# Self-attention's softmax halves exchanged by ScalarE copies instead of transfers

## The chip, the core and the metric

The kernel runs on one NeuronCore of a Trainium2 chip. The metric is the time of one execution on the device in microseconds. The engines are TensorE (matmuls; PE in the profile, PEld its weight loads), VectorE (DVE), ScalarE (ACT), GpSimd (POOL) and SyncE (SP), which here only issues DMA transfers. Each engine works through its own instructions in the order in which they were written; semaphores hold an instruction until what it needs is there.

## What is computed

One transformer block in float32 on x of 2 x 1024 x 256, with a context of 2 x 154 x 192: layer norm and self-attention with 16 heads of 64, layer norm and cross-attention to the context, layer norm and a gated feed-forward, each added to its input. Cut to what matters here:

```python
def _attention(xq, xkv, wq, wk, wv, wo, bo):
    q = (xq @ wq).reshape(B, S, N_HEADS, D_HEAD)
    k = (xkv @ wk).reshape(B, T, N_HEADS, D_HEAD)
    v = (xkv @ wv).reshape(B, T, N_HEADS, D_HEAD)
    attn = jnp.einsum('bihd,bjhd->bhij', q, k) * D_HEAD ** (-0.5)
    attn = jax.nn.softmax(attn, axis=-1)
    out = jnp.einsum('bhij,bjhd->bihd', attn, v).reshape(B, S, D_ATTN)
    return out @ wo + bo

h = _layernorm(x, ln1_g, ln1_b)
x = _attention(h, h, sa_wq, sa_wk, sa_wv, sa_wo, sa_bo) + x
h = _layernorm(x, ln2_g, ln2_b)
x = _attention(h, cond_emb, ca_wq, ca_wk, ca_wv, ca_wo, ca_bo) + x
h = _layernorm(x, ln3_g, ln3_b)
p = h @ ff_w1 + ff_b1
a, gate = p[..., :D_FF], p[..., D_FF:]
out = a * jax.nn.gelu(gate) @ ff_w2 + ff_b2 + x
```

## The kernel before

The order of the instructions on each engine is written out by hand: the program runs under a manual schedule, and each engine gets its instructions in the order in which the Python code emits them.

**Steps and units.** Self-attention runs in 16 units, one for each pair of heads (8) of each batch element (2). A unit has 8 steps; the loop over `p` counts all 128 of them. A step treats 128 queries of the pair, as two tiles of 64 queries. The 1024 keys are split into two halves, and the halves are laid on the partitions: in a tile of scores, 128 partitions by 2 heads by 512 keys, the partitions are four quarters of 32. Quarters 0 and 1 hold the same 32 queries with the first and the second half of the keys, quarters 2 and 3 the next 32 queries in the same manner (`scores`, line 476). So a softmax row lies in two neighbouring quarters, and its maximum and its sum have to be joined over both.

**The tile `st`.** For each step, `st` holds 128 partitions x [side, kind, tile, head], 2 x 2 x 2 x 2 numbers. Side 0 is what the partition's own half gave: kind 0 the negated maxima, kind 1 the sums of the exponents. Side 1 is to hold the same eight numbers of the neighbouring quarter (quarter a4 takes those of quarter a4 ^ 1). `st` has four buffers, so a step overwrites what the fourth step before it used.

**A step on the engines.** In the order of the program:

- TensorE computes the two score tiles (`s`, line 483) into two PSUM buffers, each of which can be overwritten as soon as the exponents have read it.
- VectorE takes the negated maxima of each tile (line 645, two instructions of 128 x 1024) into side 0.
- ScalarE computes the exponents (line 494, four instructions of 128 x 512, each with a read-out of the accumulated sum, which goes into side 0 as well).
- `scale_groups` of the step **before** starts with `join` (line 508). GpSimd forms the differences of the two sides' maxima (`dd`, lines 512 to 514), ScalarE their exponents (`ee`, line 516), GpSimd the joined sums (`zz`, line 518, and `den`, line 520).
- `exchange` (line 500) brings this step's side 0 to the neighbouring quarters' side 1. Its result is used by `join` one step later.
- VectorE transposes the weights of the step two before (line 609, two instructions of 128 x 1024), adds finished outputs to x in some steps (line 464), and then takes the reciprocal `rd` of the joined sums of the step before (line 591). GpSimd then scales that step's exponents by `rd` and `ee` (line 595, four instructions of 128 x 512).

The maxima of the next step are the next thing on VectorE, except that in some units the layer norm of a later stage puts statistics (lines 230 and 231) and an offset (line 246) between. On ScalarE, the instructions behind `ee` are evictions of projections or outputs from PSUM (lines 367, 375, 392, 630), and then the next step's exponents.

**TensorE's work of a step.** Behind its scores comes one of: the projection of the next unit's queries or keys (line 352) or values (line 383), a fourth of the weighted sum of the values of a finished unit half (line 530, 64 matmuls), or output projections (line 457) and small things.

**SyncE's queue.** It issues the weight loads (line 132), the regrouping of the values (lines 399 and 400), and the exchange's four transfers a step (line 504), 512 in all, each of 1 KB.

The closure in which the order of a step is written:

```python
def then():
    members = [exponents(f"{p}_{i}", sc[i], st, i) for i in range(2)]
    late = scale_groups(*joins.pop(0)) if joins else None
    exchange(st)
    joins.append((p, st, members))
    return late
```

Of the kernel before, what the change touches and what calls it, by code (L numbers as in the profile page):

```python
# [18 lines left out]
def tile_transformer_block(ctx: ExitStack, tc: tile.TileContext, a: dict, out: bass.AP):  # L19
    nc = tc.nc  # L20
# [19 lines left out]
    KB = 32  # L40
# [65 lines left out]
    for n in names[:2]:  # L106
        for r0 in range(0, P, HR):
            (nc.scalar if n == names[0] else nc.sync).dma_start(
                out=cols[r0:r0 + HR, row_of[n]:row_of[n] + NH],
                in_=w[n].rearrange("(r p) -> p r", p=HR),  # L110
# [365 lines left out]
    def scores(u, q, k, g):  # L476
        sc = ps_s.tile([P, 2, HB], F32, tag="s", name=f"s_{u}")
        for a4 in range(4):
            a2, h = divmod(a4, 2)
            for j in range(2):  # L480
                r = slice(j * DH, (j + 1) * DH)
                c = g * QG + a2 * KB
                nc.tensor.matmul(  # L483
                    sc[a4 * KB:(a4 + 1) * KB, j, :], lhsT=q[r, c:c + KB],
                    rhs=k[r, h * HB:(h + 1) * HB], start=True, stop=True,
                    tile_position=(j * DH, a4 * KB),
                )
        return sc

    def exponents(u, sc, st, i):  # L490

        pr = pp_.tile([P, 2, HB], F32, tag="P", name=f"p_{u}")
        for j in range(2):
            nc.scalar.activation(  # L494
                pr[:, j, :], sc[:, j, :], AF.Exp, bias=st[:, 0, 0, i, j:j + 1],
                accum_out=st[:, 0, 1, i, j:j + 1],
            )
        return pr

    def exchange(st):  # L500

        for a4 in range(4):
            o4 = a4 ^ 1
            nc.sync.dma_start(
                out=st[a4 * KB:(a4 + 1) * KB, 1], in_=st[o4 * KB:(o4 + 1) * KB, 0]
            )

    def join(u, st):

        dd = small.tile([P, 2, 4], F32, tag="dd", name=f"dd_{u}")  # L510
        neg = st[:, :, 0].rearrange("p s i j -> p s (i j)")
        nc.gpsimd.tensor_tensor(dd[:, 0, :], neg[:, 1, :], neg[:, 0, :], ALU.subtract)
        nc.gpsimd.tensor_tensor(dd[:, 1, :], neg[:, 0, :], neg[:, 1, :], ALU.subtract)
        nc.gpsimd.tensor_scalar(dd, dd, 0.0, 1.0, op0=ALU.min, op1=ALU.mult)
        ee = small.tile([P, 2, 4], F32, tag="ee", name=f"ee_{u}")
        nc.scalar.activation(ee, dd, AF.Exp)  # L516
        zz = small.tile([P, 2, 4], F32, tag="zz", name=f"zz_{u}")
        nc.gpsimd.tensor_tensor(zz, ee, st[:, :, 1].rearrange("p s i j -> p s (i j)"), ALU.mult)  # L518
        den = small.tile([P, 4], F32, tag="den", name=f"den_{u}")
        nc.gpsimd.tensor_tensor(den, zz[:, 0, :], zz[:, 1, :], ALU.add)  # L520
        return ee, den
# [63 lines left out]
    def scale_groups(u, st, members):  # L585

        ee, den = join(u, st)

        def reciprocals():
            rd = small.tile([P, 4], F32, tag="rd", name=f"rd_{u}")  # L590
            nc.vector.reciprocal(rd, den)  # L591
            for i, pr in enumerate(members):
                for j in range(2):
                    c = 2 * i + j
                    nc.gpsimd.tensor_scalar(  # L595
                        pr[:, j, :], pr[:, j, :], rd[:, c:c + 1], ee[:, 0, c:c + 1],
                        op0=ALU.mult, op1=ALU.mult,
                    )
                groups.append(pr)

        return reciprocals
# [35 lines left out]
    def self_first(p):  # L637

        b, pr = units[p // (2 * SH)]
        g = p % (2 * SH)  # L640
        q, k, _ = qk["sa", b, pr]
        st = small.tile([P, 2, 2, 2, 2], F32, tag="st8", name=f"st_{p}")
        sc = [scores(f"{p}_{i}", q, k, 2 * g + i) for i in range(2)]
        for i in range(2):
            nc.vector.tensor_reduce(st[:, 0, 0, i, :], sc[i], AX.X, ALU.max, negate=True)  # L645

        def then():
            members = [exponents(f"{p}_{i}", sc[i], st, i) for i in range(2)]
            late = scale_groups(*joins.pop(0)) if joins else None
            exchange(st)  # L650
            joins.append((p, st, members))
            return late

        return then
# [323 lines left out]
    with tc.manual_schedule():  # L978
# [93 lines left out]
        for c in range(CA):  # L1072
# [66 lines left out]
            elif n == 2:  # L1139
# [3 lines left out]
                elif ui == HP:  # L1143
                    wo["ca"] = const.tile([P, NPAIR, D], F32, tag="wo", name="ca_wo")
                    later[:0] = [lambda i=i: nc.sync.dma_start(
                        out=wo["ca"][:, i, :], in_=w["ca_wo"][i * P:(i + 1) * P, :])
# [65 lines left out]
```

## Time and profile before

| | us |
|---|---|
| median of 3 runs | 1120.16 (1119.69 to 1120.71) |
| the profiled execution | 1119.22 |
| its span, first to last instruction | 1117.4 |
| self-attention's steps, first maxima to last exponents | about 18.8 to 718.8 |

The stages follow one another: the first layer norm and projections up to about 18 us, the self-attention up to about 725 us (with the second layer norm beside it), then cross-attention, and the feed-forward to the end. The busy shares of the page's 40 slices (tenths; 9 is 90% or more; 28 us a slice):

```profile
PE   8999999999999999999999999999999999999998
DVE  4889999898998899999989989868777875412212
ACT  4666666766666666667666765665555553121111
POOL 2777777777777777777777777766656653220000
```

TensorE is busy throughout, VectorE nearly so in the first 26 slices, which are the self-attention; ScalarE and GpSimd are busy for about two thirds there. The costliest groups that have to do with the softmax, and the transfers of the exchange (after the count: busy time and mean duration in ns, then idle time of the engine ahead of them and what ended most of it; of a transfer: KB each, us to landing):

```profile
L494 ACT ACTIVATE p<-s,st 128x512 f32<-128x512 f32 x512 | 344.8, 686 | 199.0 <-DVE st L645 190.6
L595 POOL TENSOR_SCALAR p<-p,rd,ee 128x512 f32<-128x512 f32 x512 | 385.6, 768 | 47.6 <-DVE rd L591 46.3
L645 DVE TENSOR_REDUCE st<-s 128x2 f32<-128x1024 f32 x256 | 301.1, 1217 | 26.9 <-PE s L483 13.5
L609 DVE STREAM_TRANSPOSE pT<-p 128x1024 f32<-128x1024 f32 x256 | 302.2, 1218 | 0.3 <-POOL p L595 0.3
...
st<-st SPq DMA_DIRECT2D x512, 1.0 KB, 1.8
```

### The profile page before, as it was taken

The page shows a single profiled execution, that of the slowest core. Times are in us where ns is not written, and L with a number is a line of the kernel's source. Part 1 is how long each engine was busy: PE and PEld are TensorE (multiplying, and loading weights), DVE is VectorE, ACT ScalarE, POOL GpSimd, SP SyncE. Part 2 cuts the span into 40 slices and gives each one's busy share as a digit, 9 for nine tenths or more (in the row PEclk, how much of TensorE's full clock was granted, in tenths as well). Part 3 has the DMA queues.
Part 4 walks back from the last instruction along what each step waited for, and adds up shares of the span by engine and source line. Part 5 has one row for each costly group of instructions (what it writes and reads, how often), then busy time and mean ns, then how long its engine had stood idle before and what let it go on. Part 6 is the DMA issues. An engine that isn't in the chain of part 4 may idle for free.

```text
span 1117.4 us, 36668 instructions
## 1 busy us (share of the span) xinstructions
PE 1103.5 (99%) x14340; PEld 686.5 (61%) x14340; DVE 855.7 (77%) x1205; ACT 629.5 (56%) x2030; POOL 681.0 (61%) x1584
## 2 busy tenths in 40 slices
PE   8999999999999999999999999999999999999998
PEld 5445545545545455455455455476776777888887
DVE  4889999898998899999989989868777875412212
ACT  4666666766666666667666765665555553121111
POOL 2777777777777777777777777766656653220000
PEclk9999999999999999999999999999999999999999
DMA  3222212111111012011111111146665453000000
GB/s 85 70 57 50 55 27 51 48 34 41 32 31 42 22 41 46 13 42 39 24 41 32 31 32 26 25 95 158 160 157 125 114 115 79 10 11 10 20 10 19
DMA packets 102318, 59.14 MB, mean 53 GB/s; under 512 B 31994, under 2 KB 92930, under 8 KB 102146
## 3 DMA queue, kind: packets, MB, share of 16 engines
q1 hardware_dynamic: 100914, 56.15, 21.3%
q8 instruction: 113, 1.85, 0.7%
q10 hardware_dynamic: 1232, 0.66, 0.2%
q14 instruction: 59, 0.48, 0.1%
HBM read 27.12 MB, written 2.10 MB: 26 GB/s over the span
## 4 chain that ended last, share of the span: by engine, by line
PE 92%; ACT 2%; DVE 2%; DMA 1%; POOL 1%; SPq 1%; issue 1%; DVEq 0%; ACTq 0%; POOLq 0%
PE s L483 20%; PE po L530 20%; PE pa L933 10%; PE py_sa L457 5%; PE pv_sa L383 5%; PE py_ca L457 5%; PE pf L956 5%; PE pk_sa L352 4%; PE pq_sa L352 4%; PE pq_ca L352 4%; PE poc L851 4%; PE sc L772 3%; ACT p L494 2%; PE ph_ln L270 1%; PE pv_ca L733 1%; DVE st L645 1%
## 5 line engine op out<-in xcount | busy, mean ns | idle before, releaser
L494 ACT ACTIVATE p<-s,st 128x512 f32<-128x512 f32 x512 | 344.8, 686 | 199.0 <-DVE st L645 190.6
L595 POOL TENSOR_SCALAR p<-p,rd,ee 128x512 f32<-128x512 f32 x512 | 385.6, 768 | 47.6 <-DVE rd L591 46.3
L645 DVE TENSOR_REDUCE st<-s 128x2 f32<-128x1024 f32 x256 | 301.1, 1217 | 26.9 <-PE s L483 13.5
L609 DVE STREAM_TRANSPOSE pT<-p 128x1024 f32<-128x1024 f32 x256 | 302.2, 1218 | 0.3 <-POOL p L595 0.3
L483 PE MATMUL s<-k_sa,q_sa 64*32 64x512 f32 x4096 | 251.6, 594 | 5.0 <-ACT p L494 4.3
L530 PE MATMUL po<-pT,v_sa 64*64 64x256 f32 x4096 | 235.8, 380 | 0.9 <-DVE pT L609 0.9
L530 PEld LDWEIGHTS po<-pT,v_sa 64*64 64x64 f32 x4096 | 150.6, 133 | 109.3 <-issue 31.2
L483 PEld LDWEIGHTS s<-k_sa,q_sa 64*32 64x32 f32 x4096 | 66.8, 106 | 126.3 <-issue 68.2
L799 POOL TENSOR_SCALAR p<-p,rden 128x154 f32<-128x154 f32 x256 | 96.8, 399 | 76.0 <-DVE rden L796 75.6
L788 ACT ACTIVATE p<-sc,neg 128x154 f32<-128x154 f32 x256 | 96.1, 405 | 83.3 <-DVE rden L796 78.1
L942 DVE SCALAR_TENSOR_TENSOR u<-pa,cols,gate 128x256 f32<-128x256 f32 x64 | 31.0, 484 | 123.1 <-ACT gate L939 123.1
L933 PE MATMUL pa<-hT_ln,wf 128*128 128x256 f32 x512 | 121.1, 380 | 0.2 <-ACT p L788 0.2
L939 ACT ACTIVATE gate<-pa,cols 128x256 f32<-128x256 f32 x64 | 30.3, 474 | 147.8 <-PE pa L933 146.0
L933 PEld LDWEIGHTS pa<-hT_ln,wf 128*128 128x128 f32 x512 | 96.9, 190 | 13.9 <-issue 0.8
L494 ACT ACTIVATION_READ_ACCUMULATOR p<-s,st 128x1 f32 x512 | 103.8, 203 | 0.0
L383 PEld LDWEIGHTS pv_sa<-sa_wv,hT_ln 64*128 64x128 f32 x1024 | 58.8, 188 | 14.5 <-DMA st<-st 5.9
L518 POOL TENSOR_TENSOR zz<-ee,st 128x8 f32<-128x8 f32 x128 | 25.9, 202 | 65.6 <-ACT ee L516 65.6
L956 PE MATMUL pf<-wf,u 128*128 128x256 f32 x256 | 64.7, 379 | 0.0
L383 PE MATMUL pv_sa<-sa_wv,hT_ln 64*128 64x128 f32 x1024 | 62.0, 276 | 0.2 <-ACT v_sa L392 0.2
L457 PE MATMUL py_sa<-sa_wo,o_sa 128*128 128x256 f32 x256 | 59.7, 386 | 0.0
L457 PE MATMUL py_ca<-ca_wo,o_ca 128*128 128x256 f32 x256 | 59.7, 382 | 0.0
L457 PEld LDWEIGHTS py_sa<-sa_wo,o_sa 128*128 128x128 f32 x256 | 47.4, 190 | 17.8 <-issue 6.2
(87 smaller groups left out, 1250.6 us busy)
## 6 DMA issues: line engine op xcount, KB each, us to landing
wf<-pT_ca SPq DMA_DIRECT2D x128, 128.0 KB, 2.4
st<-st SPq DMA_DIRECT2D x512, 1.0 KB, 1.8
v_sa<-v_sa SPq DMA_DIRECT2D x32, 256.0 KB, 3.5
sa_wq<-in_L_xattn_sa_wq_dram SPq DMA_DIRECT2D x32, 128.0 KB, 2.8
sa_wk<-in_L_xattn_sa_wk_dram SPq DMA_DIRECT2D x32, 128.0 KB, 2.9
sa_wv<-in_L_xattn_sa_wv_dram SPq DMA_DIRECT2D x32, 128.0 KB, 2.9
ca_wq<-in_L_xattn_ca_wq_dram SPq DMA_DIRECT2D x32, 128.0 KB, 3.3
wf<-in_L_xattn_ff_w_dram SPq DMA_DIRECT2D x12, 256.0 KB, 4.2
```

Of the source, the lines that this page charges most:

```text
L352: nc.tensor.matmul(pq[r][f:f + m, at:at + n], lhsT=wt[own, c, f:f + m], rhs=h[own, c, t0:t0 + n], start=(c == 0), stop=(c == NH - 1), tile ...
L383: nc.tensor.matmul(pv[r][:, i * P:(i + 1) * P], lhsT=h[own, c, i * P:(i + 1) * P], rhs=wt[own, c, :], start=(c == 0), stop=(c == NH - 1), ...
L457: nc.tensor.matmul(py[:, e * D:(e + 1) * D], lhsT=o[:, i, (t + e) * P:(t + e + 1) * P], rhs=wo[kind][:, g * HP + i, :], start=(i == 0), st ...
L483: nc.tensor.matmul(sc[a4 * KB:(a4 + 1) * KB, j, :], lhsT=q[r, c:c + KB], rhs=k[r, h * HB:(h + 1) * HB], start=True, stop=True, tile_positi ...
L494: nc.scalar.activation(pr[:, j, :], sc[:, j, :], AF.Exp, bias=st[:, 0, 0, i, j:j + 1], accum_out=st[:, 0, 1, i, j:j + 1],)
L530: nc.tensor.matmul(po[a2][j * DH:(j + 1) * DH, :QH // 2], lhsT=v[r, t, e, j * DH:(j + 1) * DH], rhs=pT[r, j * NK + n, :], start=(t == 0 an ...
L595: nc.gpsimd.tensor_scalar(pr[:, j, :], pr[:, j, :], rd[:, c:c + 1], ee[:, 0, c:c + 1], op0=ALU.mult, op1=ALU.mult,)
L609: nc.vector.transpose(halves[h][:, :, c:c + KB], groups.pop(0).rearrange("p j (n k) -> p (j n) k", k=KB))
L645: nc.vector.tensor_reduce(st[:, 0, 0, i, :], sc[i], AX.X, ALU.max, negate=True)
L799: nc.gpsimd.tensor_scalar(pr_[:, j, i, :T], pr_[:, j, i, :T], rden[:, j, i:i + 1], 1.0, op0=ALU.mult, op1=ALU.mult,)
L933: nc.tensor.matmul(pa[:, half, :TF * P], lhsT=w1[:, c, half * DF + f * P:half * DF + (f + 1) * P], rhs=h[:, c, t0 * P:(t0 + TF) * P], star ...
L956: nc.tensor.matmul(sums[blk][i][:, :D], lhsT=sums[blk, "u"][:, f, i * P:(i + 1) * P], rhs=w2[:, f, :], start=(f == 0), stop=(f == NF - 1),)
```

## The change

The exchange is done by four ScalarE copies a step, each of 32 partitions by 8 numbers from one quarter to its neighbour, in place of the four transfers on SyncE's queue. The call moves up: it stands directly behind the exponents of its own step and ahead of `scale_groups` of the step before, so on ScalarE the copies come between the last exponent and `ee`. What is copied, and when it is used, stays the same.

```diff
     def exchange(st):

         for a4 in range(4):
             o4 = a4 ^ 1
-            nc.sync.dma_start(
-                out=st[a4 * KB:(a4 + 1) * KB, 1], in_=st[o4 * KB:(o4 + 1) * KB, 0]
-            )
+            nc.scalar.copy(st[a4 * KB:(a4 + 1) * KB, 1], st[o4 * KB:(o4 + 1) * KB, 0])
 
@@ self_first
         def then():
             members = [exponents(f"{p}_{i}", sc[i], st, i) for i in range(2)]
+            exchange(st)
             late = scale_groups(*joins.pop(0)) if joins else None
-            exchange(st)
             joins.append((p, st, members))
             return late
```

## The prediction

> **What bounds the kernel now.** I read the page's busy times first, then the stretches (busy time of each engine per window), then the chain that ended last, then the timeline of a few steps. A step is one pass of the loop over p in self-attention: 128 of them, between about 18 and 725 us.
>
> ```profile
> span 1117.4 us, 36668 instructions
> PE 1103.5 (99%) x14340; PEld 686.5 (61%) x14340; DVE 855.7 (77%) x1205; ACT 629.5 (56%) x2030; POOL 681.0 (61%) x1584
> 25.00:725.00 700.00, 695.73 (x11338) 365.90 (x11338) 634.19 (x705) 461.87 (x1373) 526.34 (x1181) 1.00 0.16 38
> 411.97 1.88 PE s L483 x32
> 413.85 3.43 PE pq_sa L352 x64
> 417.28 1.72 PE s L483 x32
> 419.00 3.43 PE pk_sa L352 x64
> 422.43 1.72 PE s L483 x32
> ```
>
> In the window from 25 to 725 us (the columns after the length are PE, PEld, DVE, ACT, POOL) TensorE is idle for 700.00 - 695.73 = 4.3 us. The chain there is TensorE from end to end. So TensorE sets the pace, and nothing the change does beside it can win more than about those 4.3 us in this window. From the same chain, score start to score start, the eight steps of the unit (one head pair of one batch) that begins at 411.97 take 5.31, 5.15, 5.33, 5.49, 5.65, 5.53, 5.49 and 5.49 us: 43.44 us, a mean of 5.43. The question is whether some other loop comes close to 5.43 us a step. One does:
>
> ```profile
> 242.84 0.18 DVE L591 RECIPROCAL rd<-den 128x4 f32<-128x4 f32 x1 [0.56 <-POOL den L520]
> 243.12 2.36 DVE L645 TENSOR_REDUCE st<-s 128x2 f32<-128x1024 f32 x2
> 246.95 0.21 ACT L494 ACTIVATION_READ_ACCUMULATOR p<-s,st 128x1 f32 x1
> 247.04 0.22 ACT L516 ACTIVATE ee<-dd 128x8 f32<-128x8 f32 x1
> 247.14 1.08 ACT L375 COPY k_sa<-pk_sa 128x512 f32<-128x512 f32 x2
> 247.34 0.20 POOL L518 TENSOR_TENSOR zz<-ee,st 128x8 f32<-128x8 f32 x1 [0.55 <-ACT ee L516]
> 247.62 0.20 POOL L520 TENSOR_TENSOR den<-zz 128x4 f32<-128x4 f32 x1
> 247.85 0.18 DVE L591 RECIPROCAL rd<-den 128x4 f32<-128x4 f32 x1
> 248.15 1.23 DVE L645 TENSOR_REDUCE st<-s 128x2 f32<-128x1024 f32 x1
> ```
>
> Call the start of the maxima 0 (243.12). ScalarE's exponents follow; the last read-out ends at 4.04 (246.95 + 0.21). The exponent ee of the step before starts at 3.92, zz and den follow on GpSimd, the reciprocal rd starts on VectorE at 4.73, and the next maxima, queued behind it, at 5.03. This loop goes through ee, and ee is exactly what the copies are put in front of. It takes 5.03 us against TensorE's 5.43: 0.4 us of room a step.
>
> **What the change removes.** 512 transfers, four a step, from SyncE's queue. Two prices.
>
> First, waits for their landing. In the waits:
>
> ```profile
> POOL dd L512 <- DMA st<-st: 45.8, 43, 13.7
> ACT ee L516 <- POOL dd L514: 25.2, 46, 1.4
> ACT p L494 <- DMA st<-st: 6.9, 3, 2.6
> ```
>
> (engine and line, releaser, us in total, times, longest). GpSimd waits 45.8 us, but one wait of 13.7 is its idle start, and the other 32 lie beside a TensorE that is not idle. What shows on TensorE is the ramp: at 27.18 dd waits for the first landing and ee starts 5.15 after its maxima; with local copies it would start at about 4.47, which with the values' eviction behind it brings TensorE forward by some 0.5 us. At the end of self-attention dd of the last step starts at 723.60, held by the transfer, but the scaling ahead of it on GpSimd ends only at 723.04 and itself slips by the copies: 0.2 us gained. Together 0.7 us; bounds 0 and the 4.3 above.
>
> "DMA: Bandwidth & Descriptors" of the Trainium skill (Rules for kernel authors) speaks against the change: issue a transfer early, wait for it late, and its fixed cost overlaps. By that rule the removal is worth nothing, and the total would be 0.7 us higher than the one below; the rows above agree for most steps.
>
> Second, VectorE's own waits on those transfers, before it overwrites st. In the source view, line 645:
>
> ```profile
> L645 DVEq EVENT_SEMAPHORE  x372: 21/50/921, 39.8 to 714.6; - x186
> ```
>
> Three semaphore instructions stand ahead of a step's maxima (372 over 124 steps), between rd at 247.85 and the maxima at 248.15: 0.30 us. Where an addition ahead of rd hides them, the two follow each other closely:
>
> ```profile
> 231.91 0.15 DVE L591 RECIPROCAL rd<-den 128x4 f32<-128x4 f32 x1
> 231.99 1.18 DVE L645 TENSOR_REDUCE st<-s 128x2 f32<-128x1024 f32 x1
> ```
>
> That is 0.08 us. The three cost 0.22, and without the transfers one should be left (TensorE's scores and ScalarE's copies still have to be waited for). I take 0.15 for rd to maxima, bounds 0.08 and 0.30. The gain on the loop is 0.15 us a step.
>
> **What it adds.** Four ScalarE copies of 32x8 between the last exponent and ee. No row has such a copy. Nearest: ee itself, 128x8, mean 213 ns, with the next instruction started 0.10 us behind it (247.04 to 247.14), because ScalarE overlaps neighbours. I take a pitch of 0.10, as nothing orders the four copies among themselves: the four transfers are issued 0.59 us apart with a landing of 1.8 us, so they do not wait for one another either. The bounds are 0.09 (read-out to ee, 246.95 to 247.04) and 0.24, each after the end of the one before.
>
> The first copy also reads sums that the read-outs on its own engine write, so it must wait for the last read-out to end, where ee did not. Waits of one engine on itself exist here: dd's second stage (L514) starts 0.09 after the end of its first (246.25 + 0.20 to 246.54). For ScalarE I take 0.03, its reaction to dd elsewhere (dd ends at 400.93, ee starts at 400.96), bounds -0.12 (no wait) and 0.09.
>
> So ee starts at 4.04 + 0.03 + 4 x 0.10 = 4.47 instead of 3.92, rd at 4.47 + 0.81 = 5.28 (4.73 - 3.92 = 0.81), the next maxima at 5.28 + 0.15 = 5.43. The loop grows from 5.03 to 5.43 us: just TensorE's mean. Behind ee on ScalarE stand the evictions of queries, keys and values and the output halves; they come 0.55 later, and the maxima of 1.2 us that ScalarE waits for cover most of that. Where two projections follow each other, TensorE's second waits for the first's eviction; that limits how far it can run ahead and is why I don't let it carry all its short steps below.
>
> **Sum by units.** In the eight light units (0, 5 to 8 and 13 to 15), the loop asks 8 x 5.43 = 43.44 and TensorE 43.44: +0 if TensorE may run ahead in short steps, and 0.12 + 0.28 + 0.10 = +0.5 if it never can. I take +0.25, times 8 = 2 us.
>
> In the eight units with layer-norm statistics (1 to 4, 9 to 12) VectorE has one more pair, 0.40 + 0.18 us (rows of L230 and L231), behind rd in two steps, and in one of them the offset as well (L246, 0.25): about +0.5 and +0.7 us of loop. It asks 43.44 + 1.2 = 44.6; TensorE's chain gives these units 43.4 to 44.6, mean 43.9. Carried: +0.7; never carried: 43.9 + 1.3. I take +1.0, times 8 = 8 us.
>
> Total +2 + 8 - 0.7 = +9.3 us on the profiled span: 1117.4 + 9.3 = 1126.7; 1.8 lie around the span (1119.22 - 1117.4), and the median of the runs stands 0.9 above the profiled one: 1129.5 us.
>
> **The range of this case.** The loop is close to TensorE's pace, so small errors weigh: below 5.2 us a step nothing is lost, above 5.6 every further 0.1 costs nearly 12.8 us. With pitch 0.09 and no wait for the read-out, ee starts at 4.28, the loop takes 5.24, and only the statistics steps lose: 0 to +2 us. With pitch 0.15 it takes 5.63: light units 45.0 + 0 - 43.4 = +1.6, the others 46.2 - 43.9 = +2.3, together +31. So 1120 to 1150.
>
> **Rivals.**
>
> *Copies in full one after another.* If each starts after the end of the one before (0.24 pitch), ee is at 4.04 + 4 x 0.24 = 5.00 and the loop at 5.96: (47.7 - 43.4) x 8 + (48.9 - 43.9) x 8 = 74 us, 1193. For it: busy durations of 0.21 and a shift between partitions that no row here shows. Against it: the 0.10 behind every ee. With part of it, 1150 to 1193. Chance 0.10.
>
> *The copies hide; not slower.* ScalarE has 2 us idle a step before its exponents, and TensorE covers the loop as it does now. It decides if the loop stays under about 5.2, that is if ee starts no later than 4.25. Time 1119 to 1122. Against it: ee lies behind the copies, not in that idle time. Chance 0.15.
>
> *The transfers were what cost.* Faster: late landings (the 25.2 us of ee behind dd) and the three waits go, and the ramp moves. Price at most the 4.3 us of TensorE's idle time: 1116 to 1118. It needs the loop under 5.2 as well as the whole ramp gain. Chance 0.06.
>
> My forecast has 0.69. About 0.2% (2.2 us) can be told from no change. Faster 0.06; same 0.15, the hidden case; slower 0.79. The range 1119 to 1150 leaves out the full-price rival and the faster one.
>
> **What would show it.** In the changed profile: ee 0.5 to 0.6 us behind the last exponent's read-out start; copies 0.10 apart, the first just behind the read-out's end; rd to maxima near 0.15; far fewer semaphore instructions at L645; steps near 5.43 where nothing else is on VectorE and near 6 with statistics; TensorE idle by some 10 us more between 25 and 725; maxima bound by rd, not by scores. I am wrong if copies take 0.2 each, if ee starts before 4.25, or if TensorE's own instructions change length.

## The result and the profile after

The changed kernel takes 1175.39 us (median of 4 runs, 1175.1 to 1176.4), the one before 1119.93 beside it: a ratio of 1.0498, 95% interval 1.048 to 1.0517. It is 55 us slower; I had forecast 9 us, with 1150 as the upper end.

The page of the changed kernel, first line, and its line of the chain that ended last, by engine; behind them the same line of the chain before:

```profile
span 1174.6 us, 35574 instructions
...
ACT 38%; PE 35%; DVE 14%; POOL 5%; issue 3%; DMA 0%; SPq 0%; DVEq 0%
```

```profile
PE 92%; ACT 2%; DVE 2%; DMA 1%; POOL 1%; SPq 1%; issue 1%; DVEq 0%; ACTq 0%; POOLq 0%
```

TensorE had 92% of that chain before; now ScalarE leads it. In the changed kernel's stretch from 25 to 725 us TensorE is idle for 23.1 us instead of 4.3 (columns as before; the second line is the longer stretch that self-attention now takes):

```profile
25.00:725.00 700.00, 676.88 (x10651) 342.96 (x10652) 579.49 (x653) 526.10 (x1737) 487.13 (x1088) 1.00 0.14 35
25.00:780.00 755.00, 727.71 (x11337) 367.94 (x11336) 626.23 (x704) 565.68 (x1875) 525.03 (x1172) 1.00 0.14 34
```

The idle time is only part of the loss. For practically the same matmuls (11337 against 11338) TensorE counts as busy for 727.7 us here and for 695.7 before, so some 32 us of the delay lie inside what the profile calls busy.

One turn of that chain in order of time (start, length, what; from line 506 on, line numbers are two lower than in the kernel before):

```profile
404.16 1.24 DVE st L643
...
405.42 2.80 ACT p L494 x8
...
408.23 0.20 ACT st L504
...
408.44 0.20 ACT st L504
...
408.65 0.19 ACT st L504
...
408.86 0.19 ACT st L504
...
409.07 0.22 ACT ee L514
...
409.37 0.21 POOL zz L516
...
409.65 0.21 POOL den L518
...
409.88 0.06 DVE rd L589
...
409.99 1.24 DVE st L643
```

This is the loop of the prediction, maxima to maxima, and it takes 409.99 - 404.16 = 5.83 us. Of the 108 inner steps of self-attention without statistics on VectorE, 101 now take 5.80 to 5.84. The copies start 0.21 us apart (408.23, 408.44, 408.65, 408.86), and ee starts 0.21 behind the last of them: 4.91 after the maxima's start here, 4.92 in the median over the steps, where I had 4.47.

### The profile page after: what moved, and what is told of

Its sections match the earlier page's. It is cut to its first block, busy times and chain, and to the rows that moved or that the text cites. A ratio compares the mean times of both kernels' runs of the same rounds, so it can differ in the third digit from the quotient of the medians.

```text
span 1174.6 us, 35574 instructions
## 1 busy us (share of the span) xinstructions
PE 1137.0 (97%) x14340; PEld 688.6 (59%) x14340; DVE 849.5 (72%) x1205; ACT 735.4 (63%) x2542; POOL 682.6 (58%) x1584
## 4 chain that ended last, share of the span: by engine, by line
ACT 38%; PE 35%; DVE 14%; POOL 5%; issue 3%; DMA 0%; SPq 0%; DVEq 0%
ACT p L494 27%; DVE st L643 12%; PE pa L931 9%; ACT st L504 7%; PE py_ca L457 5%; PE pf L954 5%; PE pq_ca L352 4%; PE poc L849 3%; PE sc L770 3%; PE pk_sa L352 2%; ACT ee L514 2%; POOL zz L516 2%; POOL den L518 2%; PE s L483 1%; POOL p L593 1%
## 5 line engine op out<-in xcount | busy, mean ns | idle before, releaser
L483 PE MATMUL s<-k_sa,q_sa 64*32 64x512 f32 x4096 | 276.3, 601 | 17.8 <-ACT p L494 13.4
L483 PEld LDWEIGHTS s<-k_sa,q_sa 64*32 64x32 f32 x4096 | 60.7, 105 | 166.3 <-ACT p L494 136.7
L589 DVE RECIPROCAL rd<-den 128x4 f32<-128x4 f32 x128 | 22.8, 178 | 128.1 <-POOL den L518 128.1
L504 ACT COPY st<-st 32x8 f32<-32x8 f32 x512 | 99.7, 195 | 8.5
L352 PE MATMUL pk_sa<-hT_ln,sa_wk 64*32 64x512 f32 x960 | 62.2, 592 | 7.0 <-ACT q_sa L367 7.0
```

The lines of the kernel that those rows point to most:

```text
L352: nc.tensor.matmul(pq[r][f:f + m, at:at + n], lhsT=wt[own, c, f:f + m], rhs=h[own, c, t0:t0 + n], start=(c == 0), stop=(c == NH - 1), tile ...
L483: nc.tensor.matmul(sc[a4 * KB:(a4 + 1) * KB, j, :], lhsT=q[r, c:c + KB], rhs=k[r, h * HB:(h + 1) * HB], start=True, stop=True, tile_positi ...
L504: nc.scalar.copy(st[a4 * KB:(a4 + 1) * KB, 1], st[o4 * KB:(o4 + 1) * KB, 0])
```

## Experiments

Each time stands beside the kernel before on the same chip.

| run | us | before | ratio (95% interval) |
|---|---|---|---|
| copies behind ee | 1123.36 | 1121.54 | 1.0016 (1.0006 to 1.0025) |
| transfers, call moved ahead | 1120.98 | 1121.54 | 0.9995 (0.9986 to 1.0004) |
| two copies ahead of ee, two behind | 1133.95 | 1121.54 | 1.0111 (1.0094 to 1.0128) |
| four copies of 128 partitions ahead of ee | 1124.55 | 1121.40 | 1.0029 (1.0019 to 1.0039) |
| four copies, one pair of quarters | 1135.72 | 1120.05 | 1.0137 (1.0121 to 1.0154) |
| no exchange | 1114.15 | 1121.40 | 0.9936 (0.9922 to 0.9949) |
| copies put off to the next step | 1116.29 | 1121.40 | 0.9953 (0.994 to 0.9965) |

Three more runs only measure the distance of small instructions. Their total times, one execution each, are 1126.97, 1124.94 and 1123.98 us, 3.5 to 5.4 us above the kernel before; for the first I had expected 8 to 12 us more.

### The place or the work: copies behind ee

Against the changed kernel:

```diff
-            exchange(st)
             late = scale_groups(*joins.pop(0)) if joins else None
+            exchange(st)
```

> The same four ScalarE copies a step, but behind ee instead of ahead of it. Theory (the copies lie in the loop maxima, exponents, ee, den, rd, next maxima): ee starts again about 3.9 us after the maxima, the loop takes 3.92 + 0.81 + 0.11 = 4.84 us, less than TensorE's 5.43, and the time is 1116 to 1122 us. Rival (ScalarE's load: 100 us more busy time, evictions later): ScalarE does the same work, so the time stays above 1150 us.

Measured: 1123.36 us. The same 512 copies cost 1.8 us in this place instead of 55, so ScalarE's load is not the cause of the 55 us; their place in the loop is. ee starts 3.93 us after the maxima (median over the steps), as before. The time is still 1.4 us above what I expected. The likely reason is that the evictions behind the copies come later (the run with the copies put off, below, bears this out). In the waits of this run:

```profile
PEld pk_sa L352 <- ACT q_sa L367: 16.1, 30, 1.0
```

TensorE's projection of the keys waits 30 times for the eviction of the queries, 16.1 us in total; before, it was 15 times and 5.7 us.

### The move alone: transfers ahead of the join

```diff
-            late = scale_groups(*joins.pop(0)) if joins else None
             exchange(st)
+            late = scale_groups(*joins.pop(0)) if joins else None
```

(against the kernel before, with its transfers)

> The transfers of before, with the call moved ahead of the join as in the change: the move alone. Theory: SyncE issues them when the exponents are done in either place, so 1118 to 1122 us, no difference. Rival (the place of the call costs, by semaphores that the join then waits for): slower by 0.5% or more.

Measured: 0.9995 (0.9986 to 1.0004), no difference that can be told. Moving the call costs nothing by itself.

### The dose: two copies ahead of ee

```diff
-            exchange(st)
+            exchange(st, (0, 1))
             late = scale_groups(*joins.pop(0)) if joins else None
+            exchange(st, (2, 3))
```

(against the changed kernel; `exchange` loops over the quarters that it is given)

> Two of the four copies ahead of ee, the other two behind it; all four are done. Theory (each copy ahead of ee lengthens the loop by 0.21 us): ee at 4.04 + 0.03 + 2 x 0.21 = 4.49, loop 4.49 + 0.81 + 0.11 = 5.41 us, which is the loop that the prediction had for four copies, so its sum of about +9 us holds: 1126 to 1133 us. Rival (ScalarE's load): as with all four, 1165 us or more.

Measured: ee at 4.50, and the 45 steps in which the maxima follow rd at once take 5.39 us in the median. 1133.95 us is 1 us above my range; here too the two copies behind ee hold up evictions (the keys' projection waits 23.3 us for the queries' eviction). Between none, two and four copies ahead of ee, ee starts at 3.93, 4.50 and 4.92: each copy is paid in full, and the wait for the last read-out (3.93 to 4.08) once. With two copies of 0.21 the kernel is about where I had put it with four of 0.10.

### What a small ScalarE instruction costs behind another

Three runs put rows of six small instructions on scratch tiles ahead of the kernel before. A row of the first:

```diff
+        for i in range(6):
+            a4, o4 = i % 4, i % 4 ^ 1
+            nc.scalar.copy(mb[a4 * KB:(a4 + 1) * KB, 1, i * 8:i * 8 + 8], mb[o4 * KB:(o4 + 1) * KB, 0, i * 8:i * 8 + 8])
```

> Eight rows of six small ScalarE instructions each ahead of the kernel before, to read the distance from start to start; the rest is the kernel before, some 8 to 12 us later. First idea (a shift between quarters stops the overlap): 0.21 in the shifted rows from SBUF and from PSUM, 0.10 in the rows that stay in their partitions. Second idea (reading SBUF right behind an instruction stops it): 0.21 in all rows that read SBUF, 0.10 in those that read PSUM. Third idea (only 32 partitions are at fault): 0.21 in the rows of 32 partitions, 0.10 in those of 128. Fourth idea (no small instruction overlaps another small one): 0.19 to 0.21 in all of them.

From its timeline (start, length of the whole row, engine, line, shapes): the changed kernel's copies, six that stay in their quarter but go round the quarters, and six of 128 partitions; then, with the source in PSUM, six going round the quarters and six of 128 partitions.

```profile
4.71 1.23 ACT L989 COPY mb<-mb 32x8 f32<-32x8 f32 x6
5.95 1.23 ACT L992 COPY md<-mb 32x8 f32<-32x8 f32 x6
7.20 0.69 ACT L994 COPY md<-mb 128x8 f32<-128x8 f32 x6
...
8.50 0.99 ACT L1000 COPY mq<-mp 32x8 f32<-32x8 f32 x6
9.50 0.51 ACT L1002 COPY mq<-mp 128x8 f32<-128x8 f32 x6
```

One copy lasts about 0.195 us in the first three rows. Six take 1.23 us if they start (1.23 - 0.195) / 5 = 0.207 apart, and 0.69 if they start 0.099 apart. The first idea falls (a shift is not needed), and so do the second and the fourth (rows that read SBUF, and rows of small instructions, can overlap). The third held as far as these rows go; but going round the quarters is another way to put it:

> Rows of six small ScalarE copies ahead of the kernel before: 32 partitions staying in one quarter, 32 from one quarter to another, 64 in place, 64 swapping halves, 96 in place, 32 and 128 by turns, 32 with the exponential, 128. First idea (too few partitions stop the overlap): 0.21 in every row of 32, whatever quarter; 0.10 in the row of 128; 64 and 96 are open. Second idea (a change of quarter from one instruction to the next stops it): 0.10 in the rows that keep their quarters, 0.21 only where they change.

Its rows: 32 partitions always in the same quarter; 32 always from the second quarter to the first; 64, swapping halves by turns; 96 in place; 32 and 128 by turns, both beginning at partition 0.

```profile
4.71 0.69 ACT L984 COPY md<-mb 32x8 f32<-32x8 f32 x6
5.41 0.69 ACT L986 COPY md<-mb 32x8 f32<-32x8 f32 x6
...
6.81 1.23 ACT L991 COPY md<-mb 64x8 f32<-64x8 f32 x6
8.05 0.69 ACT L993 COPY md<-mb 96x8 f32<-96x8 f32 x6
8.65 0.69 ACT L996 COPY md<-mb 32x8 f32<-32x8 f32 x6
```

Now the third idea falls too: 32 partitions overlap as well as 128, shifted or not. What costs 0.11 us more is that an instruction begins at other partitions than the one before it. (All starts tried are those of quarters: 0, 32, 64 and 96.) The last run asks which side matters, and whether other engines do the same:

> Rows of six small copies of 32 partitions ahead of the kernel before. On ScalarE: only the target's quarter changes by turns, only the source's, both, and the target's again in the upper half. Then two rows on VectorE and two on GpSimd, one each with changing and with constant quarters. Theory: 0.21 on ScalarE wherever either side changes; if only the source counts, the rows with a constant source show 0.10. For VectorE and GpSimd there is no theory: if they also overlap their neighbours, the changing row should be slower than the constant one.

On ScalarE, 0.207 us apart with only the target's quarter changing by turns (first line) and with only the source's (second):

```profile
4.71 1.24 ACT L985 COPY md<-mb 32x8 f32<-32x8 f32 x6
5.96 1.23 ACT L988 COPY md<-mb 32x8 f32<-32x8 f32 x6
```

Either side is enough. VectorE, with both sides changing and with both constant, in the same run, and GpSimd the same:

```profile
1.08 1.33 DVE L997 COPY md<-mb 32x8 f32<-32x8 f32 x6
2.43 0.53 DVE L999 COPY md<-mb 32x8 f32<-32x8 f32 x6
```

```profile
1.94 1.29 POOL L1002 COPY md<-mb 32x8 f32<-32x8 f32 x6
3.27 0.80 POOL L1004 COPY md<-mb 32x8 f32<-32x8 f32 x6
```

The starts on VectorE are 0.17 and 0.07 us apart (the first distance of the changing row, 0.48, left out), on GpSimd 0.22 and 0.12. Which side matters was not tried on these two.

### The same in the kernel

```diff
-            o4 = a4 ^ 1
-            nc.scalar.copy(st[a4 * KB:(a4 + 1) * KB, 1], st[o4 * KB:(o4 + 1) * KB, 0])
+            nc.scalar.copy(st[:, 4 - a4], st[:, 0])
...
-        st = small.tile([P, 2, 2, 2, 2], F32, tag="st8", name=f"st_{p}")
+        st = small.tile([P, 5, 2, 2, 2], F32, tag="st8", name=f"st_{p}")
```

(against the changed kernel; the exchange between the quarters is left out)

> Four copies a step in the same place, ahead of ee, but each of 128 partitions by 8 and each into its own part of a wider st; the quarters are not exchanged, each half of a row is joined with its own numbers. Theory (32-partition instructions don't overlap, 128-partition ones do): distance 0.10, ee at 4.04 + 0.03 + 4 x 0.10 = 4.47, loop 4.47 + 0.81 + 0.11 = 5.39 us, 1126 to 1133 us. Rival (it is the number of instructions in this place, and neighbours that wait for the read-outs don't overlap): 0.20 apart and 1170 us or more.

Measured: four copies ahead of ee, now 0.10 apart:

```profile
408.92 0.21 ACT L494 ACTIVATION_READ_ACCUMULATOR p<-s,st 128x1 f32 x1
409.16 0.49 ACT L503 COPY st<-st 128x8 f32<-128x8 f32 x4
409.56 0.20 ACT L513 ACTIVATE ee<-dd 128x8 f32<-128x8 f32 x1
```

ee at 4.48 and the median step 5.39 us, as expected to 0.01. The time, 1124.55, is 1.5 us below my range. The same number of instructions in the same place as in the change costs 3 us instead of 55.

The counter-test has 32 partitions again, but always the same ones:

```diff
+            nc.scalar.copy(st[:KB, 4 - a4], st[KB:2 * KB, 0])
```

(in place of the full-width copy; the join reads side 0 twice, so the exchange is left out here too)

> Four copies a step ahead of ee, each of 32 partitions by 8 as in the change, but all from the second quarter to the first, into parts of a wider st that nothing reads; the join uses each half's own numbers. Theory (a copy overlaps the one before it only if both begin at the same partitions, however many they have): copies 0.10 apart, ee 0.21 behind the last of them because it begins elsewhere, at 4.04 + 0.03 + 3 x 0.10 + 0.21 = 4.58, loop 4.58 + 0.81 + 0.11 = 5.50, 1124 to 1132 us. Rival (32 partitions in this place never overlap): 0.21 apart, ee at 4.92, 1165 us or more.

Measured:

```profile
409.15 0.49 ACT L503 COPY st<-st 32x8 f32<-32x8 f32 x4
409.66 0.21 ACT L513 ACTIVATE ee<-dd 128x8 f32<-128x8 f32 x1
```

ee at 4.59 and steps of 5.50 us, both as expected to 0.01: the copies overlap each other, and ee does not overlap the last. ee reads partitions 0 to 127, which take in the copies' source, 32 to 63; so it is where an instruction begins that counts, not whether the two share partitions. The time, 1135.72, is 4 us above my range, so near TensorE's own pace my conversion of a loop into a total is off by some us. That was not followed further.

### What the removal of the transfers is worth

```diff
             late = scale_groups(*joins.pop(0)) if joins else None
-            exchange(st)
```

(against the kernel before; the join reads side 0 twice, so the softmax of a whole row is left out)

> No exchange at all, neither transfers nor copies: each half of a row is joined with its own maxima and sums. It prices the removal of the transfers alone. Theory: TensorE's 4.3 us of idle time bound the gain, the prediction took 0.7: 1116 to 1120.5 us. Rival (late landings and the waits of VectorE on transfers cost more than the profile shows): 1114 us or less.

Measured: 0.9936, a gain of 7 us where I had 0.7, and outside the range that I gave. In the two profiled spans it is 1117.4 - 1112.3 = 5.1 us: by the starts of the maxima, 1.7 up to the first unit's end and 1.9 over the next 14 units, then 0.7 to the first scores of cross-attention and 0.9 from there to the feed-forward. The 1.9 lie where TensorE counts as fully busy in both (the kernel before, then this run):

```profile
45.00:700.00 655.00, 654.82 (x10752) 345.48 (x10737) 596.32 (x665) 430.96 (x1272) 494.24 (x1105) 1.00 0.16 38
```

```profile
45.00:700.00 655.00, 654.62 (x10770) 342.93 (x10768) 598.85 (x668) 434.50 (x1281) 494.40 (x1112) 1.00 0.15 36
```

From score start to score start, the units from the third to the last but one take 43.44 or 44.03 us here, against 43.44 to 44.71 before.

### Copies put off to the next step

```diff
         def then():
+            if joins:
+                exchange(joins[0][1])
             members = [exponents(f"{p}_{i}", sc[i], st, i) for i in range(2)]
-            exchange(st)
             late = scale_groups(*joins.pop(0)) if joins else None
```

(against the changed kernel; and once at the start of cross-attention, for the last step)

> The four copies of a step are put off to the next step, behind the evictions and directly ahead of that step's exponents, where ScalarE waits for the maxima. Theory (copies behind ee cost by holding up the evictions of the projections, 0.5 us a unit; put off, they hold up nothing): units of 43.4 to 44.0 us as before, loop 4.84 us, 1117 to 1121 us. Rival (0.83 us more of ScalarE a step cost the same wherever they stand): 1122.5 to 1125 us as with the copies behind ee.

Measured: 1116.29 us, a ratio of 0.9953: faster than the kernel before by 5 us and a little better than I expected. The copies stand behind the evictions, where ScalarE waits for the maxima:

```profile
404.19 0.81 ACT L504 COPY st<-st 32x8 f32<-32x8 f32 x4
406.77 0.69 ACT L494 ACTIVATE p<-s,st 128x512 f32<-128x512 f32 x1 [1.77 <-DVE st L643]
```

The keys' projection waits only 0.9 us, 4 times, for the queries' eviction. The time is 2 us above that of the kernel with no exchange at all.

## Why the prediction was wrong

**What bounds the kernel, and the loop: right.** TensorE set the pace at 5.43 us a step, the loop through ee stood at 5.03, and the copies lie in that loop. Between 45 and 770 us about 90% of the chain after the change is that loop; most of the rest is TensorE's projection of the keys and its scores.

**The wait for the last read-out: right.** In the turn shown above:

```profile
407.99 0.21 ACT L494 ACTIVATION_READ_ACCUMULATOR p<-s,st 128x1 f32 x1
408.23 0.81 ACT L504 COPY st<-st 32x8 f32<-32x8 f32 x4
```

The last read-out ends at 407.99 + 0.21 = 408.20, the first copy starts at 408.23, 0.03 later. It is a wait and not the change of quarter: the first copy of 128 partitions, which begins where the read-out does, keeps the same 0.03 (408.92 + 0.21 to 409.16).

**The distance of the copies: the step that failed.** "I take a pitch of 0.10, as nothing orders the four copies among themselves", said the prediction, and put 4 x 0.10 into the start of ee. The pitch is 0.207, and ee too keeps that distance (0.21). The row I took it from, ee with an eviction behind it, has two instructions that begin at the same partitions; the copies each begin at another quarter, on both sides. That the transfers don't wait for one another says that no semaphore orders the copies; it says nothing about overlap within the engine. So ee starts at 4.92 instead of 4.47, and the loop takes 5.83 instead of 5.43.

**The semaphore instructions of VectorE: right.** I took 0.15 us from rd to the maxima, with bounds of 0.08 and 0.30; it is 0.11 (409.88 to 409.99), and a third of the instructions is left, as the source view shows:

```profile
L643 DVEq EVENT_SEMAPHORE  x124: 21/50/50, 41.9 to 771.5; - x124
```

**The sum by units: right with the right distance.** With 5.83 us a step in place of 5.43, light units take 8 x 5.83 = 46.6, which is +3.2, and units with statistics 46.6 + 1.2 = 47.8, +3.9 against TensorE's 43.9. In the profile, from score start to score start, light units 6 to 8, 13 and 14 take 46.6 to 47.0 us and unit 5 takes 47.7; the ones with statistics take 47.2 to 48.2, mostly 47.9. Against the kernel before, the eight light ones are 24.5 us longer together (8 x 3.2 = 25.6 by the sum), the eight others 31.7 (31.2). Times 8 each, less 0.7: +56 us, where 55 were measured, and 57 between the two profiled spans.

The sum holds here because the loop sets every step. Near TensorE's own pace it is too high: four copies at 0.10, which is what the prediction priced, make the kernel 3 us slower by the medians and 5 by the profiled spans, not 9. One reason is a reading: 43.44 us is what one light unit takes before, where units 5 to 8, 13 and 14 take 43.4 to 44.7, so a loop of 8 x 5.43 costs them less than I took.

**The gain from the removed transfers: too small.** 0.7 us instead of 5 to 7. I had bounded it by TensorE's idle time between 25 and 725 us, but between 45 and 700 us TensorE idles for 0.2 us only and the units there still become 1.9 us shorter. The rule that the prediction cites would have made the gain nothing; the measurement decides against that. Whether the late landings cost this or VectorE's three semaphore instructions was not tried apart. It mattered little for this result: the loop sets every step, and no such gain shows in the changed kernel's units.

**The rivals and the range.** The rival with copies in full one after another is what happened, at 0.21 rather than the 0.24 that I had priced. I gave it 0.10, on the strength of one row, though I had written that no row shows a shift between partitions. A loop within 0.4 us of the bound, and four instructions of a kind that the trace lacks, with 0.09 and 0.24 as the bounds of each, call for a range up to the second.

## What to carry to other kernels

Find the loop that an added instruction lies in and compare its length with what sets the pace; here, beside the kernel with the transfers, the same copies cost 55 us in front of ee and gain 5 us in ScalarE's idle time ahead of the next exponents. A distance between instructions is a property of the pair: take it from a row whose neighbours begin at the same partitions, or at different ones, just as the added ones will. Work that is split over quarters of the partitions is best placed off the loop, or grouped so that neighbours begin at the same partition.

## What the runs showed of the hardware

On ScalarE, small copies overlap the one before only if both begin at the same partition, on the source and on the target side; the starts tried are 0, 32, 64 and 96. The distance from start to start for 32x8 float32 copies in SBUF is 0.099 us with the same partitions and 0.207 with changing ones on ScalarE. VectorE has 0.07 and 0.17 and GpSimd 0.12 and 0.22, with source and target changing together: about 0.1 us more on each. On ScalarE the number of partitions (32, 64, 96 or 128) makes no difference, and neither does a shift that stays the same. From PSUM, ScalarE's copies of 32 partitions going round the quarters start 0.167 us apart, those of 128 partitions 0.057. TensorE's busy time does not show every delay: it is 32 us longer in the changed kernel for practically the same matmuls.
